# Running sums per head on partitions, the state's product ahead of the projection, and the squares' sum behind it, in two Mamba-style mixers on one core

## The chip, the core and the metric

The kernel runs on one core of one Trainium2 chip. The metric is device time in microseconds from the first to the last instruction of the program as the runs report it; lower is better. A core has TensorE (PE, which multiplies and transposes, and whose weight loads the profile lists as PEld), VectorE (DVE), ScalarE (ACT) and GpSimd (POOL). SyncE (SP) issues DMAs. Each engine works through its own instructions in order and waits at semaphores for the others. PE writes to PSUM, which the kernel holds as eight banks of 128 partitions by 512 floats.

## What is computed

The input is 4 sequences of 1024 tokens with 512 features. Four layers follow each other, each with a residual: mixer A, a feed-forward layer, mixer B, and the same feed-forward layer again. The change is in the mixers only. One mixer, cut to what matters (A has 16 heads of width 64 with 64 states; B has 64 heads of width 16 with 128 states):

```python
proj = layer_norm(x) @ in_proj_w            # gate z, conv input (h, B, C), dt
h, B, C = silu(causal_conv4(hBC) + conv_b)  # four taps per channel
dt = softplus(dt + dt_bias)                 # one number per token and head
a  = -exp(A_log) * dt                       # decay exponent per token and head
# per head, over the tokens of a sequence:
S_t = exp(a_t) * S_(t-1) + dt_t * outer(h_t, B_t)
y_t = S_t @ C_t + D * h_t
out = (rms_norm of y and silu(z)) @ out_proj_w   # A gates first and norms then, B the other way
x = x + out
```

The kernel computes the recurrence in chunks of 128 tokens. With the running sum of a inside a chunk, cs, it needs three things from it: exp(cs_l − cs_s) between any two tokens (the matrix L), exp(cs_l) for what the state brings into the chunk, and exp(cs_last − cs_s) for what a token leaves in the state; and exp(cs_last) for the old state's own decay.

## The kernel before

**Tiles and loops.** A mixer (`mixer`, from L247) works on 32 chunks of 128 tokens, 8 per sequence, and takes two chunks as a *group* (`Group`, L374), 16 groups in all. While the chunks of one group are worked through by `chunk` (L763), the `front` (L443) of the next group is fed in between, in pieces, and the `norm` (L389) of the group after that. The order on PE, DVE, ACT and POOL is the order in which the program emits the instructions. SP's order is the scheduler's.

**The main loop** (L1005 to L1028). `chunk` is a generator: at each `yield` it names a number of microseconds, which is added to `due`, and pieces of the next front are emitted until their own numbers (1.75 for a gate, 1.9 for a convolution) have used `due` up. Emission that must come a little later is collected in `later_on` and done around the next piece.

**The front.** Its steps are listed at L605 to L629: 8 gates (`gate`, 128 gate columns by 256 tokens each; two share a PSUM tile pz, then tanh on ACT to tz, and the product z on DVE, L541) and the convolutions (`convolve`: the product pc with 259 tokens, one ACT instruction and three DVE instructions that make u, L470 to L474; `silu` then makes th on ACT and h on DVE, L494). Every such matmul goes through `large`, which afterwards emits one small piece from the list `small`: transposes of the normalized input (tpx), the eight products for dt (`project_dt`, tile pd, put at the list's head by `defer(..., True)`), and the prologue of a chunk. `finish` empties the list as far as a part that is needed now.

**dt and the sums** (`softplus`, L544 on). It runs one step at each front step from the seventh on: dt's softplus on DVE with tokens on partitions, then the exponents a, split into a rounded part and a rest (parts), then the running sums by two products with a triangle of ones on PE (pcs, L584), their two halves in float16 (two), and four DMAs to DRAM (csd, L601). `lay_sums` (L642) reads them back with SP's DMAs into past and upto, the operands of the segment sums.

**A chunk.** `prologue` (L697) gives 13 small pieces: C·B, a's product with the triangles le and gt, a's total with ones, and the transpose of B, all in one PSUM tile misc; then Gm on DVE, the exponentials ea on ACT, and Bt; then eight transposes of h (tph), each four followed by one DVE product with dt (hdt, L713) and later four ACT instructions for the skip D·h (L727). `chunk` then emits the segment sums (`decays`: seg, four PSUM tiles, exp to L on ACT, L806), a step of the previous chunk's tail, the state's product (`from_state`: po, L847, then yo on DVE with exp(cs), L851), the products on POOL that weigh hdt for the state (hdr) and decay the state S, the weighing of L by Gm on DVE (`weigh`, L813), the y blocks (`open_y`, `inner`, `close_y`: py, which first takes yo transposed), and `to_state` (pst, added to S on DVE, L909). B repeats the segment sums four times in a chunk with 16 heads each, A once.

**The tail** (`tail`, L659) of a chunk is run during the next chunk: the projection pout of eight matmuls and, between its last ones, two one-column matmuls ssq that sum the squares sq (their fold, L971 and L972, comes at the next chunk's start); then pout's copy, the root, the residual and the store.

**PSUM.** Seven banks are one pool, `mm`, for all of pz, pc, pd, pcs, pst, po, pout, ssq, misc, tph, tpx and seg. The eighth holds py. A new tile of the pool takes a bank of an earlier one and so waits for that tile's last reader.

Of the kernel before, what the change touches and what calls it, by code (L numbers as in the profile page):

```python
# [72 lines left out]
def hybrid_kernel(  # L73
# [62 lines left out]
    def load_big(tag, shape, src, name, parts):  # L136
# [19 lines left out]
    gt = const.tile([P, P], F32, tag="gt", name="gt")  # L156
    nc.gpsimd.affine_select(
        out=gt, in_=ones, compare_op=ALU.is_gt, fill=0.0, base=0, pattern=[[-1, P]], channel_multiplier=1
# [88 lines left out]
    def mixer(m, in_w, conv_w, conv_b, dt_bias, A_log, Dv, norm_w, out_w, src, dst, first, stats, last_steps={}):  # L247
# [12 lines left out]
        NE = 2 * NH + NH // SH  # L260
# [5 lines left out]
        with stack:  # L266
# [17 lines left out]
            Ab = wk.tile([P, NH], F32, tag="Ab", name=f"Ab_{m.name}")  # L284
            q.dma_start(Ab, A_log.partition_broadcast(P))
# [4 lines left out]
            dtb = wk.tile([P, NH], F32, tag="dtb", name=f"dtb_{m.name}")  # L290
            q.dma_start(dtb, dt_bias.partition_broadcast(P))
# [35 lines left out]


            sign = wk.tile([P, 1], F32, tag="sign", name=f"sign_{m.name}")
            nc.vector.memset(sign, -1.0)  # L330
            nc.vector.memset(sign[HP : 2 * HP], -LO_SCALE)
# [57 lines left out]
            def norm(f, prev):  # L389
# [35 lines left out]
                xnT = f.xnT = wk.tile([P, KD, HIST + GT], F32, tag="xnT", name=f"xnT_{tag}", bufs=3)  # L425
# [17 lines left out]
            def front(f, behind):  # L443
# [100 lines left out]
                def softplus():  # L544

                    finish(v)
                    dt = f.dt = sm.tile([P, GC, NH], F32, tag="dt", name=f"dt_{tag}")
                    nc.vector.tensor_scalar_max(dt, v, 0.0)
                    nc.vector.scalar_tensor_tensor(v, dt, -2.0, v, ALU.mult, ALU.add)
                    yield  # L550
                    exu = wk.tile([P, 512], F32, tag="t2k", name=f"exu_{tag}", bufs=4)
# [915 lines left out]
```

## Time and profile before

| what | value |
|---|---|
| median of 3 runs | 3053.41 us (3053.19 to 3053.58) |
| the profiled execution's own time | 3044.65 us |
| its span, first to last instruction | 3042.9 us |
| mean granted TensorE clock in it | 0.963 |
| mixer A, first tpx to last pout | 11.1 to 1152.9 us |
| mixer B, from the end of the first feed-forward layer | about 1342 to 2812 us |

The profile is one hardware-profiled execution. A row of a group list or a timeline names the engine, the source line, the operation, the tile written and the tiles read (buffer numbers left out), the shapes and a count. A timeline row begins with its start and its duration; what stands in brackets at its end is the idle time before it and the instruction that ended that idle time. A wait row says which instruction waited for which, and gives the total in microseconds, the number of times and the longest. A matmul in float32 is two passes, and each pass is counted; its duration reaches into the next pass's, so what passes cost is read from one start to the next.

### The profile page before, as it was taken

To read this page: it belongs to the slowest core of one execution; us is meant where nothing else is said; L and a number is where in the kernel's file an instruction comes from. 1 tells how busy PE (TensorE), PEld (TensorE's weight loads), DVE (VectorE), ACT (ScalarE), POOL (GpSimd) and SP (SyncE) were. 2 spreads that over 40 slices of the span, in tenths; PEclk is the share of its full clock that TensorE was granted. 3 is DMA by queue.
4 is the path that set the end of the run, shared out by engine and by line. 5 is a ranking of instruction groups with operands and counts; after the bars stand their busy time and mean duration, and the time that the engine had idled before them with its cause. 6 is when DMAs were issued, how large, how long until landed. Compare 5 with 4: busy or idle time off the path is not lost. (4 is left out here: it accounts for less than half of the span.)

```text
span 3042.9 us, 46127 instructions
## 1 busy us (share of the span) xinstructions
PE 2767.9 (91%) x17156; PEld 1789.5 (59%) x17156; DVE 2081.7 (68%) x4417; ACT 1261.8 (41%) x2874; POOL 720.3 (24%) x839
## 2 busy tenths in 40 slices
PE   7999999999999988999999899999888888898986
PEld 5666666666666653456666666666555565564332
DVE  5667666766666662477777687776787777875368
ACT  3334433334333332355444444444444444443245
POOL 1222122122212221351111112212222222212057
PEclk8999999999999999999999999999999999998999
DMA  3000000000000015430000000000000000001423
GB/s 117 14 19 16 16 16 17 24 17 17 16 17 22 10 68 205 154 102 10 17 20 20 13 20 18 13 17 21 22 25 21 20 23 20 13 11 72 170 88 110
DMA packets 92959, 124.25 MB, mean 41 GB/s; under 512 B 38728, under 2 KB 42328, under 8 KB 92736
## 3 DMA queue, kind: packets, MB, share of 16 engines
q1 hardware_dynamic: 80960, 98.23, 10.0%
q10 hardware_dynamic: 9792, 16.82, 1.5%
q0 software_dynamic: 1984, 6.26, 0.6%
q8 instruction: 136, 2.23, 0.3%
q14 instruction: 87, 0.71, 0.1%
HBM read 84.54 MB, written 36.72 MB: 40 GB/s over the span
## 5 line engine op out<-in xcount | busy, mean ns | idle before, releaser
L347 PE MATMUL pc_b<-xnT_b,w_in_b 128*128 128x259 f32 x1280 | 355.7, 408 | 25.1 <-DVE S_b L909 21.9
L813 DVE TENSOR_TENSOR L_b<-L_b,Gm_b 128x1024 f32<-128x1024 f32 x256 | 308.7, 1247 | 2.9 <-ACT L_b L806 2.9
L347 PE MATMUL pz_a<-xnT_a,w_in_a 128*128 128x256 f32 x1024 | 296.5, 408 | 2.9 <-ACT Bt_a L756 2.3
L347 PE MATMUL pc_a<-xnT_a,w_in_a 128*128 128x259 f32 x1152 | 299.1, 394 | 0.0
L806 ACT ACTIVATE L_b<-seg_b 128x512 f32<-128x512 f32 x512 | 263.6, 603 | 74.0 <-PE seg_b L799 74.0
L347 PE MATMUL pz_b<-xnT_b,w_in_b 128*128 128x256 f32 x1024 | 291.4, 397 | 2.9 <-ACT xnT_b L436 2.9
L474 DVE SCALAR_TENSOR_TENSOR u_b<-pc_b,cw_b,u_b 128x256 f32<-128x256 f32 x480 | 231.5, 482 | 79.8 <-ACT u_b L470 68.3
L347 PEld LDWEIGHTS pc_b<-xnT_b,w_in_b 128*128 128x128 f32 x1280 | 229.3, 198 | 92.7 <-DVE S_b L909 25.4
L474 DVE SCALAR_TENSOR_TENSOR u_a<-pc_a,cw_a,u_a 128x256 f32<-128x256 f32 x432 | 208.2, 482 | 73.6 <-ACT u_a L470 63.3
L1205 PE MATMUL g_ps<-gw,xnT_f 128*128 128x512 f32 x512 | 246.9, 619 | 9.6 <-DMA gw<-in_L_ffn_gate_w 4.2
L829 PE MATMUL py_b<-L_b,hdt_b 128*32 128x128 f32 x4096 | 165.7, 299 | 97.6 <-DVE L_b L813 96.5
L670 PE MATMUL pout_a<-w_out_a,h_a 128*128 128x512 f32 x512 | 240.2, 613 | 0.0
L670 PE MATMUL pout_b<-w_out_b,h_b 128*128 128x512 f32 x512 | 235.7, 604 | 0.0
L347 PEld LDWEIGHTS pc_a<-xnT_a,w_in_a 128*128 128x128 f32 x1152 | 200.9, 190 | 58.5 <-DVE rs_a L685 11.4
L882 POOL TENSOR_TENSOR h_b<-h_b,z_b 128x256 f32<-128x256 f32 x128 | 90.8, 730 | 509.5 <-ACT sq_b L881 509.5
L347 PEld LDWEIGHTS pz_a<-xnT_a,w_in_a 128*128 128x128 f32 x1024 | 172.3, 195 | 55.0 <-ACT out_a L679 14.4
L347 PEld LDWEIGHTS pz_b<-xnT_b,w_in_b 128*128 128x128 f32 x1024 | 174.5, 194 | 48.8 <-issue 26.0
L829 PEld LDWEIGHTS py_b<-L_b,hdt_b 128*32 128x32 f32 x4096 | 112.6, 117 | 147.7 <-DVE L_b L813 60.5
L1205 PEld LDWEIGHTS g_ps<-gw,xnT_f 128*128 128x128 f32 x512 | 93.2, 196 | 122.1 <-issue 113.5
L881 ACT ACTIVATE sq_b<-h_b 128x256 f32<-128x256 f32 x128 | 47.9, 417 | 262.5 <-DVE h_b L878 262.5
L670 PEld LDWEIGHTS pout_a<-w_out_a,h_a 128*128 128x128 f32 x512 | 93.3, 192 | 100.1 <-issue 96.3
L670 PEld LDWEIGHTS pout_b<-w_out_b,h_b 128*128 128x128 f32 x512 | 92.3, 190 | 99.5 <-issue 95.7
(321 smaller groups left out, 4919.7 us busy)
## 6 DMA issues: line engine op xcount, KB each, us to landing
d<-in_L_ffn_d_w SPq DMA_DIRECT2D x4, 2048.0 KB
x_f<-xa SPq DMA_DIRECT2D x32, 256.0 KB
xb<-x_b ACTq DMA_DIRECT2D x32, 256.0 KB
x_f<-xb SPq DMA_DIRECT2D x32, 256.0 KB
x_a<-in_L_attn_a_x SPq DMA_DIRECT2D x30, 256.0 KB
xa<-x_a ACTq DMA_DIRECT2D x30, 256.0 KB
out<-x_f SPq DMA_DIRECT2D x22, 256.0 KB
xf<-x_f SPq DMA_DIRECT2D x20, 256.0 KB
```

The lines of the kernel that those rows point to most:

```text
L347: nc.tensor.matmul(*args, **kw)
L474: nc.vector.scalar_tensor_tensor(u, ps[:, k : k + GT], cw[:, j, k : k + 1], u, ALU.mult, ALU.add)
L670: nc.tensor.matmul(pout, f.hs[e // 2][:, e % 2, cols], w_out[:, e, :], **on)
L806: nc.scalar.activation(L[:, r], sg[r0 + r], AF.Exp)
L813: nc.vector.tensor_mul(Lr, Lr, Gm.unsqueeze(1).to_broadcast([P, 2 * HB, P]))
L829: nc.tensor.matmul(py[cg * CT : (cg + 1) * CT, e % 4, :], hdt[:, h // HC, u : u + HC, :], Ls[half][:, r, hq, :], start=not started[cg], st ...
L881: nc.scalar.activation(sr, yh, AF.Square)
L882: nc.gpsimd.tensor_mul(yh, yh, zs[half * 2 + r][:, :, cols])
L1205: nc.tensor.matmul(ps, xnT[:, k, :], gw[:, k, :], start=(k == 0), stop=(k == KD - 1 and not bias_on_pe))
```

## The change

dt, its running sums and their exponentials are computed with heads on partitions (two chunks below each other, each in HP = max(heads, 32) partitions) and tokens along the free axis. The products for dt (pd) swap operands and write two column groups of one PSUM tile; ACT makes exp(−|v|) from it and DVE max(v, 0). The running sums are two scans on DVE in place of pcs. Three transposes (pt) and one ACT copy bring dt, exp(cs) and exp(rest) back to tokens on partitions (tok). The prologue loses the le and gt products and ends with one small product that picks the chunk's last row of exp(cs) (at_end), behind the turns. In the tail the squares' sum becomes a step of its own behind the projection, and `chunk` calls the tail at other places: the state's product now precedes the projection. The main loop emits a small piece where no piece of a front is left.

```diff
@@ -153,9 +153,9 @@
 nc.gpsimd.affine_select(
     out=le, in_=ones, compare_op=ALU.is_ge, fill=0.0, base=0, pattern=[[1, P]], channel_multiplier=-1
 )
-gt = const.tile([P, P], F32, tag="gt", name="gt")
+at_end = const.tile([P, P], F32, tag="at_end", name="at_end")
 nc.gpsimd.affine_select(
-    out=gt, in_=ones, compare_op=ALU.is_gt, fill=0.0, base=0, pattern=[[-1, P]], channel_multiplier=1
+    out=at_end, in_=ones, compare_op=ALU.is_ge, fill=0.0, base=1 - P, pattern=[[0, P]], channel_multiplier=1
 )
 later = const.tile([P, P], BF16, tag="later", name="later")
@@ -281,14 +286,20 @@
...
-Ab = wk.tile([P, NH], F32, tag="Ab", name=f"Ab_{m.name}")
-q.dma_start(Ab, A_log.partition_broadcast(P))
+def head_column(v, name):
+    t = wk.tile([P, 1], F32, tag=name, name=f"{name}_{m.name}")
+    if H0:
+        nc.vector.memset(t, 0.0)
+    for c in range(GC):
+        q.dma_start(t[c * HP + H0 : (c + 1) * HP], v.rearrange("(h o) -> h o", o=1))
+    return t[:R]
+Ab = head_column(A_log, "Ab")
-dtb = wk.tile([P, NH], F32, tag="dtb", name=f"dtb_{m.name}")
-q.dma_start(dtb, dt_bias.partition_broadcast(P))
+dtb = head_column(dt_bias, "dtb")
@@ -422,7 +428,7 @@
-xnT = f.xnT = wk.tile([P, KD, HIST + GT], F32, tag="xnT", name=f"xnT_{tag}", bufs=3)
+xnT = f.xnT = wk.tile([P, KD, HIST + GT], F32, tag="xnT", name=f"xnT_{tag}", bufs=XB)
@@ -494,23 +500,24 @@
...
-v = sm.tile([P, GC, NH], F32, tag="v", name=f"v_{tag}", bufs=1)
+dtT = sm.tile([P, P], F32, tag="dtT", name=f"dtT_{tag}", bufs=1)[:R]
 pds = []
-def project_dt(c, k):
+def project_dt(k):
     if k == 0:
-        pds.append(mm(f"pd_{tag}_{c}"))
-    nc.tensor.matmul(
-        pds[c][:, :NH],
-        xnT[:, k, HIST + c * P : HIST + (c + 1) * P],
-        w_in[:, k, m.dt0 : m.dt0 + NH],
-        start=(k == 0),
-        stop=(k == KD - 1),
-    )
-    if k == KD - 1:
-        nc.vector.tensor_add(v[:, c, :], pds[c][:, :NH], dtb)
-defer(v, [lambda c=c, k=k: project_dt(c, k) for c in range(GC) for k in range(KD)], True)
+        pds.append(mm(f"pd_{tag}"))
+    for c in range(GC):
+        nc.tensor.matmul(
+            pds[0][c * HP : (c + 1) * HP, :P],
+            w_in[:, k, m.dt0 - H0 : m.dt0 + NH],
+            xnT[:, k, HIST + c * P : HIST + (c + 1) * P],
+            start=(k == 0),
+            stop=(k == KD - 1),
+            skip_group_check=True,
+        )
+defer(pds, [lambda k=k: project_dt(k) for k in range(KD)], True)
@@ -543,18 +550,17 @@
...
 def softplus():
-    finish(v)
-    dt = f.dt = sm.tile([P, GC, NH], F32, tag="dt", name=f"dt_{tag}")
-    nc.vector.tensor_scalar_max(dt, v, 0.0)
-    nc.vector.scalar_tensor_tensor(v, dt, -2.0, v, ALU.mult, ALU.add)
-    yield
+    finish(pds)
+    pd = pds[0][:R, :P]
+    X = sm.tile([P, 2, P], F32, tag="X", name=f"X_{tag}", bufs=1)[:R]
     exu = wk.tile([P, 512], F32, tag="t2k", name=f"exu_{tag}", bufs=4)
-    ex, u1 = (
-        exu[:, i * GC * NH : (i + 1) * GC * NH].rearrange("p (c h) -> p c h", c=GC) for i in (0, 1)
-    )
-    nc.scalar.activation(ex, v, AF.Exp)
-    yield
+    ex, u1 = exu[:R, :P], exu[:R, P : 2 * P]
+    nc.scalar.activation(ex, pd, AF.Abs, bias=dtb)
+    nc.scalar.activation(ex, ex, AF.Exp, scale=-1.0)
+    yield
+    nc.vector.tensor_scalar(dtT, pd, dtb, 0.0, ALU.add, ALU.max)
@@ -564,41 +570,47 @@
...
-nc.vector.tensor_add(dt, dt, v)
-yield
-a = f.a = sm.tile([P, GC, NH], F32, tag="a", name=f"a_{tag}")
-nc.vector.tensor_mul(a, dt, Ab.unsqueeze(1).to_broadcast([P, GC, NH]))
-nc.vector.tensor_scalar(a, a, A_MIN * A_SCALE, 1.0 / A_SCALE, ALU.max, ALU.mult)
-parts = wk.tile([P, 512], F32, tag="t2k", name=f"parts_{tag}", bufs=4)
-parts = parts[:, : GC * 2 * HP].rearrange("p (c i h) -> p c i h", c=GC, i=2)
-if HP > NH:
-    nc.gpsimd.memset(parts, 0.0)
-hi, lo = parts[:, :, 0, :NH], parts[:, :, 1, :NH]
+nc.vector.tensor_add(dtT, dtT, v)
+yield
+a, hi = X[:, 0], X[:, 1]
+nc.vector.tensor_scalar(a, dtT, Ab, A_MIN * A_SCALE, ALU.mult, ALU.max)
+nc.vector.tensor_scalar_mul(a, a, 1.0 / A_SCALE)
 nc.vector.tensor_scalar(hi, a, A_ROUND, A_ROUND, ALU.add, ALU.subtract)
-nc.vector.tensor_sub(lo, a, hi)
-yield
-yield
-pcs = mm(f"pcs_{tag}")
-for c in range(GC):
-    nc.tensor.matmul(
-        pcs[: 2 * HP, c * P : (c + 1) * P],
-        parts[:, c, :, :].rearrange("p i h -> p (i h)"),
-        le,
-        start=True,
-        stop=True,
-    )
-rows = slice(0, 2 * HP)
-ncs = wk.tile([P, 512], F32, tag="t2k", name=f"ncs_{tag}", bufs=4)
-two = wk.tile([P, 2, GT], F16, tag="two", name=f"two_{tag}")
-nc.scalar.activation(ncs[rows, :GT], pcs[rows, :GT], AF.Identity, scale=sign[rows])
-nc.scalar.activation(two[rows, 0], pcs[rows, :GT], AF.Identity, scale=sign[rows])
-nc.vector.tensor_sub(two[rows, 1], ncs[rows, :GT], two[rows, 0])
+nc.vector.tensor_sub(a, a, hi)
+cs = wk.tile([P, 512], F32, tag="t2k", name=f"cs_{tag}", bufs=4)
+cs = cs[:R, : 2 * P].rearrange("p (i l) -> p i l", i=2)
+for i in range(2):
+    nc.vector.tensor_tensor_scan(cs[:, i], ones[:R], X[:, 1 - i], 0.0, ALU.mult, ALU.add)
+yield
+two = wk.tile([P, 2, 2, P], F16, tag="two", name=f"two_{tag}")[:R]
+scales = -1.0, -LO_SCALE
+for i in range(2):
+    nc.scalar.activation(two[:, i, 0], cs[:, i], AF.Identity, scale=scales[i])
+nc.vector.tensor_add(X[:, 0], cs[:, 0], cs[:, 1])
+nc.vector.scalar_tensor_tensor(X[:, 1], cs[:, 0], cs[:, 0, P - 1 :], cs[:, 1], ALU.subtract, ALU.add)
+yield
+for i in range(2):
+    nc.vector.scalar_tensor_tensor(two[:, i, 1], cs[:, i], scales[i], two[:, i, 0], ALU.mult, ALU.subtract)
 f.cs = dram.tile([GC, 2 * HP // 4, 2, 4, P], F16, tag="cs", name=f"csd_{tag}")
 for c in range(GC):
-    for j in range(2):
-        nc.sync.dma_start(f.cs[c, :, j], two[rows, j, c * P : (c + 1) * P])
+    for i in range(2):
+        for j in range(2):
+            nc.sync.dma_start(
+                f.cs[c, i * HP // 4 : (i * HP + NH) // 4, j], two[c * HP + H0 : (c + 1) * HP, i, j]
+            )
+nc.scalar.activation(X[:, 0], X[:, 0], AF.Exp)
+nc.scalar.activation(X[:, 1], X[:, 1], AF.Exp, bias=cs[:, 1, P - 1 :], scale=-1.0)
+yield
+yield
+pt = mm(f"pt_{tag}")
+for i, rows in enumerate((dtT, X[:, 0], X[:, 1])):
+    nc.tensor.transpose(pt[:, i * R : (i + 1) * R], rows, ident[:R, :R])
+f.tok = sm.tile([P, 3, GC, HP], F32, tag="tok", name=f"tok_{tag}", bufs=2)
+nc.scalar.copy(f.tok.rearrange("p i c h -> p (i c h)"), pt[:, : 3 * R])
@@ -664,19 +676,18 @@
 pout = mm(f"pout_{tag}")
-ssq = mm(f"ssq_{tag}")
 for e in range(KE):
     on = dict(start=(e == 0), stop=(e == KE - 1))
     nc.tensor.matmul(pout, f.hs[e // 2][:, e % 2, cols], w_out[:, e, :], **on)
-    if e >= KE - 2:
-        nc.tensor.matmul(
-            ssq[:, 0:1], sqs[0][:, e - KE + 2, :], ones[:, 0:1], start=(e == KE - 2), stop=(e == KE - 1)
-        )
 po = wk.tile([P, D], F32, tag="t2k", name=f"out_{tag}", bufs=4)
 rs = sm.tile([P, 1], F32, tag="rs", name=f"rs_{tag}", bufs=1)
+later_on.append(lambda: nc.scalar.copy(po, pout))
+yield
+ssq = mm(f"ssq_{tag}")
+for q in range(2):
+    nc.tensor.matmul(ssq[:, 0:1], sqs[0][:, q, :], ones[:, 0:1], start=(q == 0), stop=(q == 1))
 def leave():
-    nc.scalar.copy(po, pout)
     nc.vector.tensor_scalar(rs, ssq[:, 0:1], 1.0 / E, m.eps, ALU.mult, ALU.add)
@@ -732,33 +743,37 @@
     misc = got["misc"]
     if q == 0:
         nc.tensor.matmul(misc[:, :P], f.Bc[:, cols], f.Cc[:N, cols], start=True, stop=True)
-    elif q < 3:
-        nc.tensor.matmul(
-            misc[:, P + (q - 1) * NH : P + q * NH], (le, gt)[q - 1], f.a[:, c, :], start=True, stop=True
-        )
-    elif q == 3:
+    elif q == 1:
+        nc.tensor.transpose(misc[:, P : P + N], f.Bc[:, cols], ident[:N, :N])
+        later_on.append(spread)
+    else:
         for i in range(SH):
+            h0 = H0 + i * NS
             nc.tensor.matmul(
-                misc[i * N : i * N + N, P + 2 * NH : P + NE],
-                ones[:, :N],
-                f.a[:, c, i * NH // SH : (i + 1) * NH // SH],
+                misc[i * N : i * N + N, P + N : P + N + NS],
+                at_end[:, :N],
+                f.tok[:, 1, c, h0 : h0 + NS],
                 start=True,
                 stop=True,
                 skip_group_check=True,
             )
-    else:
-        nc.tensor.transpose(misc[:, P + NE : P + NE + N], f.Bc[:, cols], ident[:N, :N])
-        Gm = wk.tile([P, P], F32, tag="Gm", name=f"Gm_{tag}", bufs=2)
-        nc.vector.tensor_mul(Gm, misc[:, :P], le)
-        ea = sm.tile([P, NE], F32, tag="ea", name=f"ea_{tag}", bufs=2)
-        nc.scalar.activation(ea, misc[:, P : P + NE], AF.Exp)
-        Bt = wk.tile([P, N], F32, tag="Bt", name=f"Bt_{tag}", bufs=2)
-        nc.scalar.copy(Bt, misc[:, P + NE : P + NE + N])
-        f.early[c] = Gm, ea, Bt
-return [lambda q=q: sums_of(q) for q in range(5)] + [
-    lambda half=half, q=q: turn(half, q) for half in range(2) for q in range(4)
-]
+        et = sm.tile([P, NS], F32, tag="et", name=f"et_{tag}", bufs=2)
+        nc.scalar.copy(et, misc[:, P + N : P + N + NS])
+        f.early[c] = *got["GB"], et
+def spread():
+    misc = got["misc"]
+    Gm = wk.tile([P, P], F32, tag="Gm", name=f"Gm_{tag}", bufs=2)
+    nc.vector.tensor_mul(Gm, misc[:, :P], le)
+    Bt = wk.tile([P, N], F32, tag="Bt", name=f"Bt_{tag}", bufs=2)
+    nc.scalar.copy(Bt, misc[:, P : P + N])
+    got["GB"] = Gm, Bt
+return (
+    [lambda q=q: sums_of(q) for q in range(2)]
+    + [lambda half=half, q=q: turn(half, q) for half in range(2) for q in range(4)]
+    + [lambda: (catch_up(), sums_of(2))]
+)
@@ -767,14 +782,14 @@
 tag = f"{m.name}_{i}"
 cols = slice(c * P, (c + 1) * P)
 begin, end = ci == 0, ci == NCH - 1
-hs, zs, a, Bc, Cc = f.hs, f.zs, f.a, f.Bc, f.Cc
+hs, zs, Bc, Cc = f.hs, f.zs, f.Bc, f.Cc
 past, upto = pasts[i % 2], sums[i % 2]
 last = state["tail"]
 hdt = hdts[i % 2]
 finish(f)
-Gm, ea, Bt = f.early[c]
-el, er, et = ea[:, :NH], ea[:, NH : 2 * NH], ea[:, 2 * NH :]
+Gm, Bt, et = f.early[c]
+el, er = f.tok[:, 1, c, H0:], f.tok[:, 2, c, H0:]
 if c + 1 < GC:
     defer(f, prologue(f, c + 1))
@@ -911,9 +926,9 @@
 state.pop("fold", lambda: None)()
 L0 = decays(0)
-next(last, None)
 if not begin:
     from_state()
+next(last, None)
 if not end:
     hdr = wk.tile([P, E], F32, tag="hdr", name=f"hdr_{tag}")
     nc.gpsimd.tensor_mul(
@@ -936,6 +951,7 @@
 py, on = open_y(0)
 for half in range(2):
     inner(0, L0, half, py, on)
+next(last, None)
 L2 = decays(2)
 yield 3.0
 weigh(L2)
@@ -958,6 +974,7 @@
 next(last, None)
 yield 2.5
 to_state()
+next(last, None)
 yield 2.0
 for half in range(2):
     py, on = open_y(half)
@@ -1018,6 +1035,11 @@
     for step in waiting:
         step()
     if piece is None:
+        if small:
+            small.pop(0)()
+            due -= 0.35
+            continue
         break
     due -= piece
 catch_up()
```

More of the change, by code (lines that the diff above doesn't have):

```diff
@@ L259, in mixer @@
         SW = E // SH
-        NE = 2 * NH + NH // SH
+        H0 = HP - NH
+        R = GC * HP
+        NS = NH // SH
+        XB = 2 if NH > 16 else 3
         def state_at(half):
@@ L326, in mixer @@
                     nc.gpsimd.memset(t, 0.0)
-            sign = wk.tile([P, 1], F32, tag="sign", name=f"sign_{m.name}")
-            nc.vector.memset(sign, -1.0)
-            nc.vector.memset(sign[HP : 2 * HP], -LO_SCALE)
             gc = 0.5 * m.mup_z
@@ L544, in softplus @@
                 def softplus():
[L546 to L556 removed]
+                    finish(pds)
+                    pd = pds[0][:R, :P]
+                    X = sm.tile([P, 2, P], F32, tag="X", name=f"X_{tag}", bufs=1)[:R]
+                    exu = wk.tile([P, 512], F32, tag="t2k", name=f"exu_{tag}", bufs=4)
+                    ex, u1 = exu[:R, :P], exu[:R, P : 2 * P]
+                    nc.scalar.activation(ex, pd, AF.Abs, bias=dtb)
+                    nc.scalar.activation(ex, ex, AF.Exp, scale=-1.0)
+                    yield
+                    nc.vector.tensor_scalar(dtT, pd, dtb, 0.0, ALU.add, ALU.max)
+                    v = X[:, 0]
                     nc.vector.tensor_scalar_add(u1, ex, 2.0)
@@ new lines, in softplus @@
+                    for i in range(2):
+                        nc.vector.scalar_tensor_tensor(two[:, i, 1], cs[:, i], scales[i], two[:, i, 0], ALU.mult, ALU.subtract)
+                    f.cs = dram.tile([GC, 2 * HP // 4, 2, 4, P], F16, tag="cs", name=f"csd_{tag}")
+                    for c in range(GC):
+                        for i in range(2):
[3 more added lines that the diff above has]
+                                )
@@ L598, in softplus @@
-                    f.cs = dram.tile([GC, 2 * HP // 4, 2, 4, P], F16, tag="cs", name=f"csd_{tag}")
-                    for c in range(GC):
-                        for j in range(2):
-                            nc.sync.dma_start(f.cs[c, :, j], two[rows, j, c * P : (c + 1) * P])
+                    pt = mm(f"pt_{tag}")
+                    for i, rows in enumerate((dtT, X[:, 0], X[:, 1])):
+                        nc.tensor.transpose(pt[:, i * R : (i + 1) * R], rows, ident[:R, :R])
+                    f.tok = sm.tile([P, 3, GC, HP], F32, tag="tok", name=f"tok_{tag}", bufs=2)
@@ L715, in turn @@
                         tp.rearrange("p (n u d) -> p n u d", u=HC, d=HD),
-                        f.dt[:, c, half * HALF : (half + 1) * HALF]
+                        f.tok[:, 0, c, H0 + half * HALF : H0 + (half + 1) * HALF]
                         .rearrange("p (n u) -> p n u", u=HC)
```

## The prediction

> **What bounds the kernel.** I read the page's busy shares first, then busy time by stage, PE's waits inside the two mixers, and timelines of single groups.
>
> ```profile
> span 3042.9 us, 46127 instructions
> PE 2767.9 (91%) x17156; PEld 1789.5 (59%) x17156; DVE 2081.7 (68%) x4417; ACT 1261.8 (41%) x2874; POOL 720.3 (24%) x839
> ...
> PE   7999999999999988999999899999888888898986
> ```
>
> TensorE is full but for about a tenth. The stages differ, though (window, length, then busy us by engine):
>
> ```profile
> 94.00:700.00 606.00, 581.98 (x3096) 392.60 (x3092) 406.18 (x960) 234.47 (x584) 125.51 (x166) 0.98 0.06 18
> ...
> 1427.00:2120.00 693.00, 642.14 (x4872) 437.58 (x4871) 505.90 (x984) 309.84 (x719) 123.13 (x140) 0.97 0.06 18
> ```
>
> Mixer A leaves PE 24 us idle in 606, B 51 in 693, and DVE is 67% and 73% busy. PE's waits from 94 to 1100 us (A), then from 1427 to 2640 us (B), each with its total, how often, and the longest:
>
> ```profile
> PE ssq_a L672 <- DVE sq_a L972: 28.8, 14, 2.7
> PE py_a L860 <- DVE h_a L878: 7.9, 15, 1.0
> ...
> PE py_b L829 <- DVE L_b L813: 79.2, 56, 5.8
> PE pc_b L347 <- DVE S_b L909: 18.2, 10, 2.0
> ```
>
> So A is bound by PE's own work plus one wait of 2.1 us per group of two chunks, the squares' sum; B waits for DVE to weigh L. Here is that stretch of A, on PE and then on DVE:
>
> ```profile
> 437.11 5.53 PE L347 MATMUL pc_a<-xnT_a,w_in_a 128*128 128x259 f32 x24
> 442.57 0.62 PE L789 MATMUL seg_a<-later,ident 64*64 64x256 bf16 x8
> 443.12 0.39 PE L799 MATMUL seg_a<-upto,past 21*128 21x512 f16 x4
> 443.45 6.28 PE L670 MATMUL pout_a<-w_out_a,h_a 128*128 128x512 f32 x14
> 451.91 0.35 PE L672 MATMUL ssq_a<-ones,sq_a 128*128 128x1 f32 x2 [2.18 <-DVE sq_a L972]
> 452.12 1.10 PE L670 MATMUL pout_a<-w_out_a,h_a 128*128 128x512 f32 x2
> 453.06 0.28 PE L672 MATMUL ssq_a<-ones,sq_a 128*128 128x1 f32 x2
> 453.27 1.13 PE L847 MATMUL po_a<-S_a,Cc_a 64*128 64x512 f32 x4
> 454.33 1.99 PE L347 MATMUL pz_a<-xnT_a,w_in_a 128*128 128x256 f32 x8
> ```
> ```profile
> 443.28 0.17 DVE L548 TENSOR_SCALAR dt_a<-v_a 128x32 f32<-128x32 f32 x1
> ...
> 445.94 1.52 DVE L474 SCALAR_TENSOR_TENSOR u_a<-pc_a,cw_a,u_a 128x256 f32<-128x256 f32 x3 [2.26 <-ACT u_a L470]
> ```
>
> Steps start to start (a 128x512 pass of pout 0.43 us, a pz or pc pass 0.217) are what PE pays; the printed durations overlap.
>
> **The change, part by part.** Let P be the start of the second y block of a group's first chunk (435.53 above), and a group two chunks, about 71 us in A and 88 to 95 in B. There are 16 groups per mixer; the 15 that have a successor count.
>
> *Order in the tail, A.* Before: P+7.9 the projection (pout), P+16.4 the squares' sum after 2.18 us of waiting, P+17.7 the state's product (po), P+18.8 the next gate. The change puts the sum past a later conv, so 2.18 goes, and two detours of some 0.2 us. But po now stands right behind the segment sums, with nothing between. A PSUM tile takes the bank released earliest among seven; with dt's bank one instead of two and held longer, the changed program gives the odd chunk's po banks whose last readers are the conv chain of tile 2 and the max that makes dt. In the DVE rows that conv chain ends at 445.94+1.5 = P+11.9 (ACT's work behind it gets slightly shorter: I take P+11.1); the max comes next, P+11.8. Before, 7 us of pout covered exactly this. PE arrives at P+7.9, so about 3.9 us of stall (bounds 2.5 and 5); everything queued on PE stands behind it: pout, the gates, the next conv. Then po 1.06, pout 6.9: the gate starts near P+19.8, **+1.0 us per group** (+0.9 to +1.45). Without a stall it would be P+15.9, −2.9. In the even chunk po waits for the hdt muls, pout for the ACT copy behind eight skips (2.43 us): 0.3 to 0.5, set against its shorter prologue.
>
> *dt's product.* Before, 8 matmuls; a pz pair with its pd pair steps 0.655 (487.04, 487.71, 488.37), a pz pair alone 0.433: 0.22 each, 1.78 per group. After, four steps of two column tiles. Nearest row: L741, also two 64-wide column tiles amid pz. It begins 0.09 later behind its pz pair than L736 does (475.64 to 476.25 against 474.98 to 475.50), its passes fit in 0.22, and what follows takes 0.1 more: 0.41 per step. Against this speaks a rule of the Trainium skill, "TensorEngine Tiling (Array Packing)", Key Properties: switching the tiling mode drains TensorE. A drain, estimated from the trace, is a pass's duration less its step, 0.408−0.217 = 0.19; two of them and 0.22 make 0.60. By the row the four steps cost 1.64, by the rule 2.40; I take 0.55, 2.2 per group: +0.42. The row is short of one switch here, since a 64-wide tile followed, hence nearer the rule.
>
> *Prologue.* Since dt takes four places instead of eight in the first two gates' matmuls, four later pieces of the second chunk's prologue move up into gate 1: C·B (0.59 in A, 0.33 in B), the B transpose (0.40, 0.11) and two turns of 0.11. They leave a stretch after gate 1 that DVE bounds (z, three convs of 1.52, h), where their absence gains nothing, for one that PE bounds: +1.2 in A, +0.66 in B. The removed le and gt products (4 of 0.22 per group) earn their half outside the DVE stretch. Outside lie 0.44 and a tail detour of 0.2, less the even chunk's wait of 0.4 above: −0.25. A, from the last y block to gate 1: +0.42 +1.2 −0.25 = **+1.4**.
>
> *Running sums.* PE loses pcs (463.58 to 464.16, 0.58) and gains three transposes, no row, between three turns (0.33) and three switched ones (0.9): 0.6 taken; with changed bank order **+0.2** per group. The sums themselves go to DVE as two scans; no row has one, and the nearest, a 128x128 operation of 0.29, bounds it below, a 0.95 reciprocal above. In A the polynomial also grows from 32 to 128 columns (0.2 to 0.29, the reciprocal 0.35 to 0.95), about +1.5 with the scans +0.8. That lies in DVE's idle time before yo, which waits for po (110.8 us in 26 waits in A), unless that has moved. SP issues 8 DMAs per group for the sums instead of 4 (0.77 each), each half as large and one step earlier; behind them stand the loads for the next segment sums, due about when they land. I take 0, and up to +1 per group if the issues don't shrink. ACT's Abs is new: a table load is 1.28 us in this trace (L311), and two per group would cost 82 us in all. The skill's "ScalarE: Activation LUTs", Table sets, says abs is in every set; the trace, which has four loads in all but no Abs, cannot tell. I take none.
>
> *B.* The stretch from gate 1 is DVE's. There goes ACT's exp of the sums waiting behind DVE's Gm (42.9 us in 26 waits before), which held what DVE did next by about 1.1 per group, with two adds: −1.1. In the tail: pout's detours (about 0.2 each) and the le/gt pair (0.44), less a 0.3 wait for the B transpose's copy: −0.4; but in the 6 groups that carry residual steps po meets a conv's bank, +0.4 instead. Running sums +0.15; last stretch +0.66 +0.1 −0.75 ≈ 0. So −1.3 for 9 groups and −0.9 for 6.
>
> *Set-up.* Two columns per head vector in place of a broadcast row are four small loads and two memsets per mixer, made beside the weights' loads; xnT drops to two buffers in B, where only a group and the one behind it are alive. Nothing for either; a late release of xnT would show as ACT's copy waiting.
>
> *Ends.* Small pieces now fill the last group's idle places (one gap before 1117 us is 4.3), and B's first front loses a 2.8 wait for pcs against a later pt: −5 together.
>
> *Sum.* A: (1.0+0.2+1.4)×15 = +39. B: −17. Ends −5. **+17 us** on the profiled execution's 3044.65, its own time, 1.75 more than its span; 3062. The median of three runs is 8.8 higher; so 3070.
>
> **Rivals.**
> - *The po banks are free in time* (faster). If tile 2's conv and the max are done by P+8, A gives −2.9+0.2+1.4 = −1.3 ×15 = −20, B −17, ends −5: −42, **3011**. It turns at a stall of 2.8 us where I have 3.9. For it: DVE idles 2.26 us before that conv, waiting for ACT alone; with less queued on ACT that goes. Against: ACT's xn there waits for DVE, and Abs and Exp are added ahead.
> - *DVE comes due* (slower still). A's 2.3 us more DVE per group lands between conv and sum in the PE-bound stretch, the squares' fold and yo slip, and B's odd po waits 1.5 in every group: +2.3×15 = 35 more, **3105**. Decides once the scans and polynomial outlast the idle before yo (about 4.3 per wait).
> - *No change*: A's new stalls and B's gains cancel, stall 2.8: **3053**.
> - *All savings arrive*: the moved prologue pieces cost nothing and the le/gt products count in full. A −2.9+0.42−0.88 = −3.4, ×15 = −50; B −17 and 0.66×15 = 10 more; ends −5: −82, **2971**.
>
> **Chances.** Change is told from no change at 0.2%, 6 us. My forecast (3060 to 3092) 0.42; DVE due 0.13; no change 0.12; banks free 0.24; all savings 0.09. So faster 0.33, same 0.12, slower 0.55. The forecast's own range is 3060 to 3092; 8 in 10 runs from 3005 to 3108: it leaves out the all-savings case and the far end of DVE's.
>
> **What would show it.** PE waiting for u of tile 2 or dtT ahead of po in A's odd chunks, 3 to 4 us, some 14 times; no wait at ssq; pout right behind po. If this wait is under 2 us, the forecast is wrong, and the time is near 3011. The four dt steps read as 2.2 us per group between gates 0 and 1, with C·B ahead of gate 1's end. In B the wait of py for L in its group's last chunk should shrink from 79 us, the one for S_b stay. If ACT shows more than four table loads, or scans longer than 1 us, the slower rival holds.

## The result and the profile after

The changed kernel takes **3193.13 us** (median of 4 runs, 3184.88 to 3195.73) against 3053.49 us for the kernel before on the same chip: a ratio of 1.0449 between the means, 95% interval 1.0427 to 1.0470. The forecast was 3070, so 17 us more; it is 140 more. The profiled execution took 3184.88 us.

The page of the changed kernel, then two stages of it (window, length, busy us by engine, granted TensorE clock as third number from the end):

```profile
span 3183.0 us, 45741 instructions
PE 2813.3 (88%) x16868; PEld 1731.7 (54%) x16868; DVE 2146.5 (67%) x4479; ACT 1278.3 (40%) x3002; POOL 738.6 (23%) x823
```
```profile
100.00:706.00 606.00, 559.71 (x2805) 355.75 (x2804) 402.90 (x926) 222.26 (x569) 116.44 (x148) 0.95 0.05 16
1508.00:2201.00 693.00, 627.77 (x4659) 407.63 (x4655) 504.31 (x977) 305.22 (x739) 136.66 (x140) 0.97 0.06 17
```

PE has fewer instructions than before and is busy longer. In the stretch of A its clock is 0.95, where it was 0.98, and it stands idle for 46 us of 606 instead of 24. Its waits in A (100 to 1170 us) and in B (1508 to 2790 us) of the changed kernel:

```profile
PE po_a L862 <- DVE u_a L480: 48.4, 14, 4.3
PE py_a L875 <- DVE h_a L893: 17.0, 26, 1.6
...
PE py_b L844 <- DVE L_b L828: 54.0, 41, 5.5
PE pc_b L353 <- DVE S_b L924: 27.9, 10, 3.0
...
PE po_b L862 <- DVE u_b L480: 10.6, 6, 2.4
PE pout_b L681 <- ACT L_b L821: 10.0, 5, 2.4
```

The wait for the squares' sum is gone from A, and the forecast wait at po is there, 14 times, 3.5 us each. The same stretch of A as in the prediction, timeline of PE, changed kernel:

```profile
462.31 5.53 PE L353 MATMUL pc_a<-xnT_a,w_in_a 128*128 128x259 f32 x24
467.77 0.62 PE L804 MATMUL seg_a<-later,ident 64*64 64x256 bf16 x8
468.33 0.40 PE L814 MATMUL seg_a<-upto,past 21*128 21x512 f16 x4
472.35 2.56 PE L862 MATMUL po_a<-S_a,Cc_a 64*128 64x512 f32 x4 [3.63 <-DVE u_a L480]
474.85 8.94 PE L681 MATMUL pout_a<-w_out_a,h_a 128*128 128x512 f32 x16
483.62 2.32 PE L353 MATMUL pz_a<-xnT_a,w_in_a 128*128 128x256 f32 x10
```

Read the starts. po now takes 474.85−472.35 = 2.50 us for four passes, which took 1.06 before; pout takes 8.77 for sixteen, forecast at 6.9. That is **3.3 us more for the same work**, right behind the wait. Busy time by window in the same place shows why (the third number from the end again):

```profile
468.00:472.30 4.30, 0.72 (x12) 0.23 (x8) 1.55 (x4) 3.44 (x10) 0.00 (x0) 0.93 0.00 0
472.30:474.85 2.55, 2.50 (x5) 1.00 (x5) 2.41 (x8) 2.30 (x5) 0.00 (x0) 0.50 0.00 0
...
479.00:481.00 2.00, 2.00 (x6) 0.85 (x5) 1.97 (x5) 0.00 (x0) 0.00 (x0) 1.00 0.00 0
```

The clock falls to half when PE has stood idle, and comes back to 1.00 while PE works. A stall of 3.6 us costs 6.9 here.

The kernel before is not free of this. Its clock fell in 7 of the 14 groups in which A waited for the squares' sum, each time behind that wait (1.8 to 2.7 us). Timeline of PE in such a group, kernel before:

```profile
379.61 0.56 PE L672 MATMUL ssq_a<-ones,sq_a 128*128 128x1 f32 x2 [2.73 <-DVE sq_a L972]
...
382.23 2.08 PE L847 MATMUL po_a<-S_a,Cc_a 64*128 64x512 f32 x4
384.24 3.27 PE L347 MATMUL pz_a<-xnT_a,w_in_a 128*128 128x256 f32 x10
```

From start to start po takes 2.01 us here. The prediction worked with a group in which the clock stayed up.

For the runs below a mixer's time is taken from its first tpx to its last pout on PE; a group's period from one dt product to the next. Two more sums come from the trace: PE's idle time, and the time at half clock, half of which is lost if PE is busy in it.

| mixer | us before | after | PE idle | at half clock |
|---|---|---|---|---|
| A | 1142.4 | 1211.9 | 60.1 to 100.0 | 64.9 to 112.6 |
| B | 1471.2 | 1536.8 | 140.6 to 195.4 | 129.4 to 150.2 |

So A's 69.5 are 40 of idle time, up to 24 of clock, and some 6 of added work; B's 65.6 are 55 of idle time and up to 10 of clock. The second feed-forward layer did not change; the stretch between the mixers grew by 5.3 us (188.5 to 193.8), which no run takes apart.

### The profile page after: what moved, and what is told of

Read it like the earlier page. It is cut to its first block, busy times and chain, and to the rows that moved or that the text cites. A ratio compares the mean times of both kernels' runs of the same rounds, so it can differ in the third digit from the quotient of the medians.

```text
span 3183.0 us, 45741 instructions
## 1 busy us (share of the span) xinstructions
PE 2813.3 (88%) x16868; PEld 1731.7 (54%) x16868; DVE 2146.5 (67%) x4479; ACT 1278.3 (40%) x3002; POOL 738.6 (23%) x823
## 5 line engine op out<-in xcount | busy, mean ns | idle before, releaser
L353 PE MATMUL pc_b<-xnT_b,w_in_b 128*128 128x259 f32 x1280 | 365.5, 418 | 48.5 <-DVE S_b L924 33.0
L828 DVE TENSOR_TENSOR L_b<-L_b,Gm_b 128x1024 f32<-128x1024 f32 x256 | 301.2, 1219 | 2.2 <-ACT L_b L821 2.2
L353 PEld LDWEIGHTS pc_b<-xnT_b,w_in_b 128*128 128x128 f32 x1280 | 237.5, 204 | 117.3 <-DVE S_b L924 39.2
L353 PE MATMUL pz_a<-xnT_a,w_in_a 128*128 128x256 f32 x1024 | 282.2, 400 | 1.6 <-ACT et_a L761 0.9
L353 PE MATMUL pz_b<-xnT_b,w_in_b 128*128 128x256 f32 x1024 | 278.5, 396 | 4.3 <-ACT xnT_b L442 4.3
L681 PE MATMUL pout_a<-w_out_a,h_a 128*128 128x512 f32 x512 | 252.5, 650 | 0.0
L844 PE MATMUL py_b<-L_b,hdt_b 128*32 128x128 f32 x4096 | 155.5, 289 | 61.9 <-DVE L_b L828 60.8
L681 PEld LDWEIGHTS pout_a<-w_out_a,h_a 128*128 128x128 f32 x512 | 104.2, 210 | 154.5 <-issue 150.4
L681 PEld LDWEIGHTS pout_b<-w_out_b,h_b 128*128 128x128 f32 x512 | 99.7, 196 | 141.9 <-issue 124.6
L223 POOL TENSOR_TENSOR rs_b<-rs_b,neg_half 128x1 f32<-128x1 f32 x32 | 43.9, 1373 | 536.5 <-DVE rs_b L691 536.5
```

The source lines that it names most:

```text
L223: nc.gpsimd.tensor_tensor(v, v, neg_half[: v.shape[0]], ALU.pow)
L353: nc.tensor.matmul(*args, **kw)
L681: nc.tensor.matmul(pout, f.hs[e // 2][:, e % 2, cols], w_out[:, e, :], **on)
L828: nc.vector.tensor_mul(Lr, Lr, Gm.unsqueeze(1).to_broadcast([P, 2 * HB, P]))
L844: nc.tensor.matmul(py[cg * CT : (cg + 1) * CT, e % 4, :], hdt[:, h // HC, u : u + HC, :], Ls[half][:, r, hq, :], start=not started[cg], st ...
```

## The experiments

Two explanations were set against each other. Theory C: the order of the tail costs, through PSUM banks and the clock. Theory D: the heads' part costs. Each table row is one run against the kernel before on its own chip, with the ratio's 95% interval; A and B are from one profiled execution each, and the changed kernel's code gave B as 1532.9, 1536.8 and 1542.7 (e5, the change, e13), so less than 10 us in one mixer tells little.

| run | us (before there) | ratio | A | B |
|---|---|---|---|---|
| e1 heads, old tail | 3171.4 (3052.2) | 1.0347 to 1.0431 | 1206.5 | 1527.5 |
| e2 new tail alone | 3118.4 (3052.2) | 1.0181 to 1.0249 | 1186.7 | 1499.3 |
| e3 change, pieces out of gate 1 | 3147.0 (3052.2) | 1.0279 to 1.0338 | 1193.5 | 1515.6 |
| e4 change, dt's bank freed | 3140.8 (3052.2) | 1.0259 to 1.0318 | 1199.6 | 1508.2 |
| e5 change, wait filled | 3155.7 (3065.4) | 1.0229 to 1.0351 | 1181.2 | 1532.9 |
| e6 e1, dt's bank freed | 3157.3 (3065.4) | 1.0251 to 1.0339 | 1217.7 | 1503.2 |
| e7 e6, pieces out of gate 1 | 3146.5 (3065.4) | 1.0226 to 1.0293 | 1206.2 | 1506.1 |
| e8 e7, sum behind po | 3018.2 (3065.4) | 0.9785 to 0.9898 | 1128.3 | 1446.0 |
| e9 e8, po first | 3125.5 (3057.0) | 1.0179 to 1.0285 | 1190.0 | 1498.6 |
| e10 before, sum behind po | 3015.9 (3057.0) | 0.9831 to 0.9916 | 1109.4 | 1473.0 |
| e11 e8, dt's bank held | 3099.2 (3057.0) | 1.0102 to 1.0189 | 1185.4 | 1477.9 |
| e12 e8, pieces in gate 1 | 3026.1 (3057.0) | 0.9879 to 0.9924 | 1138.9 | 1448.3 |
| e13 change, wait half filled | 3175.9 (3055.4) | 1.0360 to 1.0423 | 1193.8 | 1542.7 |
| e14 A of e10, B of e8 | 2996.4 (3055.4) | 0.9784 to 0.9830 | 1108.5 | 1452.2 |

**Each half alone: e1, e2.** e1 is the changed kernel with the old tail; e2 is the reverse of this edit, on the kernel before:

```diff
-                if not begin:
-                    from_state()
                 next(last, None)
+                if not begin:
+                    from_state()
...
+                    if e >= KE - 2:
+                        nc.tensor.matmul(
+                            ssq[:, 0:1], sqs[0][:, e - KE + 2, :], ones[:, 0:1], start=(e == KE - 2), stop=(e == KE - 1)
+                        )
...
-                yield
-                ssq = mm(f"ssq_{tag}")
-                for q in range(2):
-                    nc.tensor.matmul(ssq[:, 0:1], sqs[0][:, q, :], ones[:, 0:1], start=(q == 0), stop=(q == 1))
...
-                    next(last, None)
```

> The changed kernel with its tail put back: the squares' sum between the last matmuls of the projection, the state's product behind the projection, the residual's steps at their old places; dt and the running sums stay on heads. Theory C (the tail's order costs: po and pout need three PSUM banks right behind the segment sums, PE waits about 3.6 us for them once per group of A, and the TensorE clock then stays at half for 6.8 us, another 3.3 us): no PE wait at po_a, one slow clock stretch per group gone from A, A's groups back from 75.1 to about 70 us, B's groups with residual steps from 102 to about 96; total 3050 to 3090. Theory D (the heads part costs: dt's bank held long, four prologue pieces moved into gate 1, more DVE work): A's groups stay above 73 us, total above 3140.

> The kernel before with the tail's part of the change alone: the state's product ahead of the projection, the squares' sum as its own step behind it; dt and sums as before. Theory C: in the odd chunks of A po waits for the conv chains of tiles 1 and 2, about 3 us, with half clock after it; in B the residual comes later and leaves DVE idle ahead of a conv; total 3110 to 3170. Theory D: 3035 to 3065.

D's numbers came true in e1 and C's in e2, so neither theory is enough alone: each half by itself makes most of the loss in A (64 and 44 of 69.5). PE's waits in A (100 to 1200 us), e1 then e2:

```profile
PE pout_a L682 <- DVE u_a L480: 47.9, 14, 4.3
...
PE po_a L846 <- DVE u_a L474: 38.2, 13, 3.6
```

It is the same wait for the conv of tile 2 in both; only who stands in it differs. With the old tail it is pout, because dt's bank is still held by the heads' part and no bank is free. With the new tail it is po, because po's two banks and pout's are asked for at once (e6 and e9 below bear on the two). The prediction named both causes and took them for one; either is enough.

**Two smaller parts: e3, e4.** e3 adds four empty places behind dt's steps; e4 copies dt's product out of PSUM when it is complete. First e3's edit, then e4's:

```diff
-                defer(pds, [lambda k=k: project_dt(k) for k in range(KD)], True)
+                defer(pds, [lambda k=k: project_dt(k) for k in range(KD)] + [lambda: None] * 4, True)
```
```diff
+                    if k == KD - 1:
+                        nc.vector.tensor_scalar(dtT, pds[0][:R, :P], dtb, None, ALU.add)
...
-                    nc.scalar.activation(ex, pd, AF.Abs, bias=dtb)
+                    nc.scalar.activation(ex, dtT, AF.Abs)
...
-                    nc.vector.tensor_scalar(dtT, pd, dtb, 0.0, ALU.add, ALU.max)
+                    nc.vector.tensor_scalar_max(dtT, dtT, 0.0)
```

> The changed kernel with four empty places behind dt's four steps, so that the four prologue pieces (C.B, the transpose of B, two turns) come behind gate 1 again. Theory C: these pieces cost 1.2 us per group in A and about 1 in B, where z and all that follows on DVE comes later by them: minus 15 to minus 35 us in all, 3158 to 3178. Theory D, if these pieces are the main cost: minus 60 or more. If the period of A is held at 22 windows of the clock (75.09 us), A does not move at all and only B gains, about minus 12.

> The changed kernel with dt's product copied from PSUM to SBUF by one DVE instruction as soon as it is complete, so that its bank is free long before the segment sums of the odd chunk. Theory C: po still needs the bank of tile 2's conv, so the wait ends at P+11.1 instead of P+11.8 and the clock still drops: 3175 to 3195. Theory D (the long hold of dt's bank is the cause): the wait at po_a and the slow clock stretch in A go, minus 90 or more, below 3100.

Against the kernel before, e3 loses 95 and e4 89 where the change loses 140; that is 45 gained (A 18, B 21) and 51 (A 12, B 29), both more than theory C said and less than D. In A they match C: po still waits in e4. e3's third case, a period of A that the clock holds fast, is ruled out: A moved. In B both shorten the first stretch of a group by 2 us or more (dt's product to pst, in most groups without residual steps: 18.6 to 20.2 in the change, 16.4 and 16.3 here, 14.8 before).

**Is the clock a cause or a companion: e5, e13.** In A's odd chunks PE gets idle matmuls to do while it waits, 14 or 7; they are read by nobody:

```diff
+                if c % 2 == 1 and CG == 2:
+                    idle = p_y.tile([P, 4, P], F32, tag="y", name=f"idle_{tag}")
+                    for n in range(14):
+                        nc.tensor.matmul(
+                            idle, ident16, later.unsqueeze(1).to_broadcast([P, 4, P]), start=True, stop=True, skip_group_check=True
+                        )
                 if not begin:
                     from_state()
```

> The changed kernel with 14 idle matmuls (128x512, bfloat16, into the y bank, read by nobody) in A's odd chunks between the segment sums and po, where PE waits 3.6 us; they take about 3.0 us and end before the banks of po come free. If the slow clock after the wait is caused by the wait itself (PE idle), po and pout run at full clock again although more work was added: A's groups from 75.1 to about 71.8 us, minus 40 to minus 55, 3138 to 3155. If the slow stretch comes from what runs there (po, pout, power) and not from the idle time: 3190 to 3205.

> As e5 with 7 idle matmuls instead of 14, some 1.5 us of work, so that PE still waits about 2.1 us in front of po in A's odd chunks. If the clock drops by how long PE is idle at a stretch (2.2 us ahead of the squares' sum did not drop it in the kernel before, 3.6 us did in the change): the clock stays full, mixer A takes 1178 to 1190 us as in e5 (1181.2), against 1211.9 in the change. If any wait there drops it, or if it is the drained operand queue: 1200 to 1215.

e5, timeline of PE in such a chunk, and busy time by window behind the wait:

```profile
455.63 3.20 PE L932 MATMUL idle_a<-later,ident 128*128 128x512 bf16 x14
459.34 1.62 PE L862 MATMUL po_a<-S_a,Cc_a 64*128 64x512 f32 x4 [0.52 <-DVE u_a L480]
```
```profile
459.00:463.00 4.00, 3.66 (x9) 1.65 (x10) 3.83 (x10) 2.36 (x5) 1.24 (x2) 1.00 0.00 0
```

More work makes the kernel faster: the clock stays at 1.00, most of A's groups take 72.7 us instead of 75 to 76, mixer A is 30.7 shorter and its time at half clock 23.9 instead of 112.6. So idle time is the cause. With 7 matmuls (e13) PE waits 26.6 us in 13 times, about 2.0 each, and the clock falls in 7 of 14 groups; A is 18.1 shorter, between the two expectations. So waits of about 2 us drop the clock half the time, as in the kernel before; what the expectation says of that kernel holds for half of its groups. The waits of 3.1 to 4.3 us in the change dropped it in all 14 groups.

**Freeing the bank under the old tail: e6, e7.** e1 with e4's edit; then with e3's too.

> Heads on partitions with the tail put back (as e1) and dt's bank freed by one DVE copy (as e4). e1's odd chunks of A wait 52 us for a bank in front of pout, and po would not need one before the L exponentials. Bank theory: with dt's bank free pout starts at once, the wait and the slow clock after it go: A's groups 70 to 71.5 us, total 3060 to 3085. If the bank is not what matters: above 3140.

> e6 with the prologue pieces behind gate 1 again (as e3). By e3 another minus 15 to minus 40: 3025 to 3060. If e3 gained only because it moved the wait against the clock's windows, no further gain: within 8 us of e6.

The bank was what pout waited for, and the time did not come. Timeline of PE, e6:

```profile
469.09 6.28 PE L683 MATMUL pout_a<-w_out_a,h_a 128*128 128x512 f32 x14
479.81 0.35 PE L685 MATMUL ssq_a<-ones,sq_a 128*128 128x1 f32 x2 [4.44 <-DVE sq_a L989]
...
481.53 2.08 PE L864 MATMUL po_a<-S_a,Cc_a 64*128 64x512 f32 x4
483.53 2.72 PE L353 MATMUL pz_a<-xnT_a,w_in_a 128*128 128x256 f32 x10
```

pout starts at once, and PE waits at the squares' sum instead, 60.7 us in 15 times where the kernel before had 28.8 in 14; then again at half clock (po 2.00 where 1.06 is full). On DVE the heads' part has put more of the polynomial ahead of the squares' fold, which starts 5.7 us behind the conv of tile 2 in e6 and 2.9 before. That is the prediction's second rival, "DVE comes due". In the change it is hidden, since the sum comes later there. e7's further gain of 11 is in A alone and outside both expectations.

**The sum behind, po behind: e8, then one edit each: e9, e11, e12; and e10 on the kernel before.** e8 is e7 with the change's form of the tail, and these calls in `chunk` (A has its third call where the change has it):

```diff
                 next(last, None)
                 if not begin:
                     from_state()
+                if CG == 4:
+                    next(last, None)
```

e9 moves `from_state` ahead of the first of these calls; e11 takes out e4's edit, e12 e3's; e10 is this tail on the kernel before.

> Heads on partitions, dt's bank freed, prologue pieces behind gate 1, projection ahead of the state's product as in the kernel before, and the squares' sum still behind: in A as in the change, in B right behind po so that the residual keeps its old place. A loses its 28.8 us of waiting for the sum: 2990 to 3035, faster than the kernel before. If po's first bank (that of tile 2's conv) binds behind pout, or if the sum's new place costs what it saves: within 10 us of e7.

> e8 with one edit, the state's product ahead of the projection again. e8 was 47 us faster than the kernel before on its chip. Bank theory: three banks are asked for behind the segment sums in A's odd chunks, po waits for the convs of tiles 1 and 2 for about 3.2 us at P+8, and the clock is halved behind it: A's groups from 69.7 to 73 to 75.5 us; between 10 us faster and 55 us slower than the kernel before. If the order of po and pout is harmless once dt's bank is free: within 10 us of e8, that is 37 to 57 faster than before.

> The kernel before (dt and sums with tokens on partitions) with nothing but the squares' sum behind the projection, placed as in e8. If e8's gain is the sum's place alone: 30 to 50 us faster than the kernel before. If the heads part carries it: within 12 us of the kernel before, in either direction.

> e8 without the copy that frees dt's bank. Bank theory: as in e1, pout in A's odd chunks waits about 3.5 us for the conv of tile 2, and the clock halves: 40 to 110 us slower than e8, from 7 faster to 60 slower than the kernel before. Rival (bank held does no harm when the sum is behind): within 10 us of e8.

> e8 with the four prologue pieces in gate 1, as in the change. From the working of the prediction 1.2 us per group in A; from e3 about 1 in B: 15 to 35 us slower than e8. If they cost only where a wait behind them crosses into the slow clock: within 8 us of e8.

e8 is faster than the kernel before by 1.0 to 2.2%. From there each part of the change shows its price alone (A and B): po first +61.7 and +52.6; dt's bank held +57.1 and +31.9; pieces in gate 1 +10.6 and +2.3, which is within the scatter (e12 is 8 us above e8, but their ratio intervals overlap). PE's waits in A (100 to 1200 us) of e9, and (100 to 1160 us) of e11:

```profile
PE po_a L863 <- DVE u_a L480: 37.2, 13, 3.8
...
PE pout_a L681 <- DVE u_a L480: 51.5, 14, 4.6
```

Timeline of PE, e9, shows how many banks there are behind the segment sums:

```profile
460.51 1.12 PE L863 MATMUL po_a<-S_a,Cc_a 64*128 64x512 f32 x2
464.55 2.04 PE L863 MATMUL po_a<-S_a,Cc_a 64*128 64x512 f32 x2 [2.91 <-DVE u_a L480]
```

One bank is free: po's first half takes it, and the second waits for the conv. With the projection first, pout takes it, and its 7 us cover the conv.

In B the three add up to 86.8 of the 90.8 between e8 and the change. In A they make 129 and the change has 83.6: there po first and the held bank end in one and the same wait. e9's loss exceeds its range by 13; its expectation names A's groups only, and B lost 52.6, by the groups' periods 35 of it in the 6 groups with residual steps. e10, without any head on partitions, is as fast as e8, so the sum's place is enough for such a gain. By mixer the two differ: e10's 33 us are all in A, where the wait for the sum is gone and the time at half clock falls from 64.9 to 37.5; e8 gains 14 in A and 25 in B.

**Each mixer as it is shorter: e14.** A as in e10, B as in e8.

> Mixer A as in e10 (dt and sums with tokens on partitions, squares' sum behind), mixer B as in e8 (heads on partitions, dt's bank freed, pieces behind gate 1, squares' sum behind). If the stages are separable: A 1109 (e10) and B 1446 (e8), minus 1 and minus 27 us against the better of e10 and e8 in each stage: 2985 to 3000, a ratio of 0.976 to 0.984. If the heads' gain in B comes from what A leaves behind: about 3015.

2996.4 us, 1.7 to 2.2% under the kernel before, A within 1 us and B within 7 of the runs they come from. Heads on partitions cost A 19 us (e8 against e10) and gain B 21 to 27 (e14 and e8 against e10).

## Why the prediction was wrong

The sum had A at +39, B at −17 and the ends at −5. Measured are +69.5 in A, +65.6 in B and +5.3 between the mixers, so B is the larger miss.

**The wait at po, right.** Forecast 3.9 us in A's odd chunks from P+7.9 to P+11.8; in the timeline above P is 460.73, po starts at P+11.6 after 3.63.

**What it costs, wrong: the step "Then po 1.06, pout 6.9".** I priced the passes behind the stall at the durations of passes that follow full work. They measure 2.50 and 8.77. The gate starts at P+22.9 instead of P+19.8, so +4.1 per group where +1.0 stood. In the same group of e5, where the wait is filled, po starts at P+11.6 too, and the gate at P+20.2: the 2.7 between are the clock. That e5's mixer A ends 38.8 above the kernel before, where the sum had +39, is in part luck: e5 also lacks most of the clock loss that the kernel before has (23.9 us at half clock against 64.9), and that makes up for terms that came out larger. The trace of before had the evidence, in A in 7 of 14 groups (above) and in B (timeline of PE, kernel before):

```profile
2316.67 1.08 PE L829 MATMUL py_b<-L_b,hdt_b 128*32 128x128 f32 x32
...
2325.02 2.22 PE L829 MATMUL py_b<-L_b,hdt_b 128*32 128x128 f32 x32 [5.32 <-DVE L_b L813]
```

The same 32 passes take twice as long after a wait of 5.3 us. I had read only the one 2.18 at the squares' sum, behind which the passes ran at full rate. The Trainium skill gives the rule in "TensorE: Matmul & The Clock Gate", section "Why this matters for your kernels": no idle gaps of more than some 3 us between bursts of matmuls, or the clock goes back to half. The change agrees, as waits of 3.1 to 4.3 us dropped it every time; but shorter ones, 1.5 to 2.7 us, dropped it in half of the groups of e13 and of the kernel before, and the measurement decides: 3 us is no safe bound here.

**A's other terms, nearly right.** Running sums, forecast +0.2 per group for their stretch: 16.35 against 16.18. dt's step, forecast 0.55: gates with dt step 0.97, alone 0.433, so 0.54, on the side of the tiling rule (0.60) rather than the row (0.41). The last stretch, forecast +1.4: 23.8 against 21.8, +2.0, all of it between dt's first product and the end of gate 1, so the −0.25 outside did not come. The 0.6 beyond the forecast are some 9 us in 15 groups. The pieces in gate 1, forecast 1.2: 1.2 by e3, 0.7 by e12. Table loads stayed four, with Abs in use; two scans take 0.73 together, inside the bounds. No wait for past or upto appears, so SP's four more DMAs show no cost.

**B, wrong: the step "−1.3 for 9 groups and −0.9 for 6".** By the groups' periods, measured are +0.8 to +3.9 (2.7 on average) and +4.9 to +10.0 (7.7). The gains that it counted did come: e8, with heads on partitions, has B 25 us shorter than the kernel before. What it priced at next to nothing is the tail's order (−0.4, and +0.4 where residual steps are carried) and dt's held bank (no term at all). po first costs 52.6 (e9) and the held bank 31.9 (e11). In the 6 groups with residual steps PE waits at po and then at pout for banks (10.6 and 10.0 us in all, so 1.8 and 2.0 at a time), and pout can follow at half clock: 8.64 us for sixteen passes in one of them. The sign that was named came in part: the wait of py for L went from 79.2 to 54.0 us, but the one for S, which should have stayed, from 18.2 to 27.9.

The step also let every new wait of PE vanish because "the stretch from gate 1 is DVE's". But what DVE does there starts from PE: dt's steps and the pieces in gate 1 moved z by 1.1 us (5.48 behind dt's first product before, 6.54 in the change, 6.10 in e3). And the residual, which used to fill DVE's time until the first conv came, now comes behind the sum and so behind the next weighing. Timeline of DVE, changed kernel:

```profile
1983.21 1.52 DVE L480 SCALAR_TENSOR_TENSOR u_b<-pc_b,cw_b,u_b 128x256 f32<-128x256 f32 x3 [1.36 <-ACT u_b L476]
...
1987.91 0.75 DVE L697 SCALAR_TENSOR_TENSOR x_b<-out_b,rs_b,x_b 128x512 f32<-128x512 f32 x1
```

DVE stands for 1.36 us where the residual's instructions were, and does them later on the same chain. That this costs much is not shown: e9 leaves the residual at its old place, and e9, e11 and e12 together make up all but 4 us of B's loss against e8. How the price of po first and that of the held bank divide between waits, clock and DVE's order in B was not tried.

**The rivals.** "Banks free in time" did not come; the stall's own length was as forecast, but what it sets off was missing. "DVE comes due" was real in A, as e6 shows, but covered by the sum's new place. No rival had the clock, and none let two causes each be sufficient.

## What to carry to other kernels

Price an idle stretch of TensorE in front of full work by what follows it as well: here one of 3.6 us cost nearly twice its length, and one of 2 us cost 1.7 us more in half of the cases. Look in the trace for passes of one shape with two durations before summing, and sort the groups by whether the clock fell before taking one as typical. When an operation is moved ahead, count the PSUM banks that are asked for at its new place and who frees each; two parts that lean on the same bank look like one cause and must be undone together. And price a move in every stage that has it: in B, where po first seemed harmless, it cost 52.6 us.

## What the runs showed of the hardware

The time at half clock comes in stretches that are multiples of 3.41 us. In the changed kernel's A they last 6.83 us, and fourteen in a row begin 75.09 us apart (22 times 3.41), though single groups take 72.6 to 76.0 us from one dt product to the next. It looks as if the groups' period were held to the clock's own step, but e3 speaks against it: with the pieces out of gate 1 A became 18.4 us shorter, and its stretches began 20 to 22 steps apart. Each begins a whole number of steps after the last in both. With the wait filled (e5) most groups took 72.7 us, and between 60 and 1150 us one stretch of 3.41 was left. How long a wait must be to drop the clock is not one number: the shortest that did was 1.2 us (e5, once), and many of about 2 us did not.
